# Attention scores by seven products, with their sums accumulated in two kept PSUM banks, a fused sum and maximum on VectorE, and one more pair of tiles

## The chip, the cores and the metric

The kernel runs on one core of one Trainium2 chip. The metric is the device time of one execution in microseconds (us). The engines are PE (TensorE, matrix products into PSUM), DVE (VectorE), ACT (ScalarE), POOL (GpSimd) and SP, whose queue issues most DMAs. Each engine works through its own instructions in order and waits at semaphores for the others. [...]

## The reference

The input x has 2 sequences of 2048 tokens with 512 features. With xn = layernorm(x), the output is

```
x + attention(xn) * silu(moe(xn))
```

`attention` normalises again, forms q, k, v with a 512x1536 matrix, takes causal softmax(q k^T / sqrt(512)) v with one head of width 512, multiplies by o_proj and adds its input. `moe` sends each token to the best 2 of 8 experts (512 to 352 to 512, with silu) and adds the two results with their softmax weights. All is fp32.

## The kernel before, in words

There are three stages: projections of all tokens with the expert routing, the experts, and the attention with the output. The change touches the third and the places where the second and third take PSUM banks.

The whole program is emitted under a manual schedule: every engine's instructions stand in the order in which the Python code emits them. So the order of the calls is the order of the queues, and it is by reading the calls that one sees what stands behind what.

**Attention.** A tile is 128 queries; there are 32, taken in the order `seq` (step number s = 0 to 31): the first sequence from its last tile to its first, then the second sequence in a mixed order. The keys of a sequence lie in 4 blocks of 512, and a tile needs the blocks up to its own, the last one masked. A chunk (s, j) is the scores of tile s against block j: `chunk_scores` (L1214) multiplies over the 512 features in 4 parts, masks the diagonal (L1224) and takes the row maximum (`maximum`, L1204). `end_scores` (L1305) makes nm, the negated maximum over a tile's chunks. `exponentials` (L1377) then runs exp on ACT for each piece, straight from the PSUM bank of a chunk or from the SBUF tile `turned[s]`, and sums the rows on the way. The exponentials are transposed by a split copy on POOL (L1394, `pu`), a DMA transpose (L1400, `puT`) and a join on DVE (`join_p`, L1414); the shortest tiles (`by_te`, at most 3x128 keys) are transposed on PE instead (`turn_p`, L1407), into a bank of kind "a".

**Seven products.** For pairs of tiles in `SCORED` (s//2 in 0, 1, 2, 3, 13, 14, 15), the scores of two tiles against blocks 0 and 1 are done by the Winograd form of Strassen's scheme: 2x2 parts, 7 products instead of 8, in `fast_scores` (L1254). It needs sums of the queries (`query_sums`, L1232, 4 sums in tile `sq`) and of the key blocks (`block_sums`, L1243, 4 sums in tile `tk`, once per sequence). Each product is two fp32 matmuls of 128x512 (the profile shows 4 PE instructions) into a bank of its own; the sums of products are made by DVE (L1277) in `turned[s]` and `turned[s+1]`, whose first 1024 columns are c11, c12 and c21, c22. The copy of product 1 is on ACT (L1290), at s=2 on DVE (L1288). `others` emits work that the caller hands in, such as `attended` and `join_p`.

**PSUM.** Two pools: `ps_b` with 3 banks, `ps_a` with 5, each used in turn. "a" holds the chunks (kept until their exponentials), PE's transposes and the experts' first products; "b" the values and the experts' second products. The products of `fast_scores` take from both.

**Around it.** In a step s the main loop emits, in this order where they apply: late work of earlier tiles (`attended`, ACT L1595 and DVE L1598), the sums of the next pair's queries, `fast_scores`, the chunks, joins, `values(s-2)` with `turn_p(s-1)`, `end_scores`, `combine_p`, `divisor` (L1556, waits for the exponentials of tile s-1), `exponentials`, the DMAs of `fetch_parts`, the work in `later` (`block_sums` and `combine_v` for the second sequence), the value products (`FAST` pairs use seven products here too), and, in odd steps from 3 on, `gate` (L1582: two ACT scalings L1587, two DVE sums L1588, a Silu L1590).

Of the kernel before, what the change touches and what calls it, by code (L numbers as in the profile page):

```python
# [20 lines left out]
P = 128  # L21
# [5 lines left out]
def gated_attention_moe(  # L27
# [962 lines left out]
    def up(i):  # L990
        ev = experts[i] = expert(places(i)[0][1], mybir.EngineType.PE)
        xT = xts.pop(i)
        ph = ps_a.tile([P, TB], F32, name=f"ph_{i}", tag="a")[:, :H]
# [40 lines left out]
    def up_pair(i, meanwhile):  # L1034
        ev = experts[i] = experts[i + 1] = expert(order[i], mybir.EngineType.PE)
        (a11, a12), (_, a22) = ([xts[i + k][:, 2 * j : 2 * j + 2] for j in range(2)] for k in range(2))
        s1, s2, s3, s4 = xsums.pop(i)
        hs = [hp.tile([P, H], F32, name=f"h_{i + k}", tag="h") for k in range(2)]
        (c11, c12), (c21, c22) = ([h[:, ts(j, H2)] for j in range(2)] for h in hs)

        def b(r, j):
            return lambda c: w1[0][:, bass.ds(ev, 1), 2 * r + c, ts(j, H2)]

        def t(k):
            return lambda c: w1s[0][:, bass.ds(ev, 1), k - 1, c, :]

        def made(x, y):
            ps = ps_a.tile([P, TB], F32, name="p7", tag="a")[:, :H2]
# [49 lines left out]
    def down(i):  # L1098
        ht = hts.pop(i)
        ev = experts.pop(i)  # L1100
        py = ps_b.tile([P, D], F32, name=f"py_{i}", tag="b")
# [78 lines left out]
    OUT = 4  # L1180


    SCORED = (0, 1, 2, 3, 13, 14, 15)
    FAST = SCORED + (4,)

    def place(s):
        b, t = divmod(seq[s], BT)
# [2 lines left out]
    def begin_scores(s):  # L1190
        b, t, first = place(s)
        widths[s] = [TB] * (b - first) + [(t + 1) * P]
        mx = sm.tile([P, NBB], F32, name=f"mx_{s}", tag="mx")
        nm = sm.tile([P, 1], F32, name=f"nm_{s}", tag="nm")
        scored[s] = mx, nm, []

    def room(s):

# [2 lines left out]
        )  # L1201
        turned[s] = tp.tile([P, longest], F32, name=f"pT_{s}", tag=f"pT{s % 4}", bufs=1)

    def maximum(s, src, at):  # L1204

        mx, _, pieces = scored[s]
        nc.vector.tensor_reduce(mx[:, len(pieces) : len(pieces) + 1], src, AX.X, ALU.max)
        pieces.append((src, at))

    def direct(s):  # L1210

        return range(2 if s // 2 in SCORED else 0, len(widths[s]))

    def chunk_scores(s, j):  # L1214
        b, t, first = place(s)
        w = widths[s][j]
        ps = ps_a.tile([P, TB], F32, name=f"ps_{s}_{j}", tag="a")
        for c in range(ND):
            nc.tensor.matmul(  # L1219
                ps[:, :w], lhsT=aqs[seq[s] // 2][:, c, ts(t % 2, P)], rhs=aks[first + j][:, c, :w],  # L1220
                start=(c == 0), stop=(c == ND - 1),
            )
        if first + j == b:
            nc.vector.tensor_tensor(ps[:, w - P : w], ps[:, w - P : w], keep, ALU.min)  # L1224
        maximum(s, ps[:, :w], j * TB)

# [24 lines left out]
                engine = nc.gpsimd if i == 3 and first == 0 else nc.vector  # L1251
                engine.tensor_tensor(k[:, i - 1], x1, x2, ALU.subtract)

    def fast_scores(s, pools, meanwhile=()):  # L1254

        first = place(s)[2]
        (a11, a12), (a21, a22) = (
# [3 lines left out]
        q, k = qsums.pop(s), bsums[first]  # L1261
        (c11, c12), (c21, c22) = ([turned[s + i][:, ts(j, TB)] for j in range(2)] for i in range(2))
        meanwhile = list(meanwhile)
        count = [0]

        def made(x, y):
            pool, tag = pools[count[0] % len(pools)]
            count[0] += 1
            ps = pool.tile([P, TB], F32, name=f"p7_{s}_{count[0]}", tag=tag)
            for c in range(ND // 2):  # L1270
                nc.tensor.matmul(  # L1271
                    ps, lhsT=x[:, c], rhs=y[:, c], start=(c == 0), stop=(c == ND // 2 - 1)
                )
            return ps

        def add(out, x, y):
            nc.vector.tensor_tensor(out, x, y, ALU.add)  # L1277

        def others(n):
            while meanwhile and n:  # L1280
# [1 line left out]
                f(*args)  # L1282
                n -= 1

        p1 = made(a11, b11)
        if s == 2:

            nc.vector.tensor_copy(c11, p1)  # L1288
        else:
            nc.scalar.copy(c11, p1)  # L1290
        p2 = made(a12, b21)
        add(c12, made(q[:, 1], k[:, 1]), c11)
        add(c11, p2, c11)
        add(c21, made(q[:, 2], k[:, 2]), c12)
        p5 = made(q[:, 0], k[:, 0])
        add(c22, p5, c21)
        add(c12, p5, c12)
        others(1)
        add(c12, made(q[:, 3], b22), c12)
        maximum(s, turned[s][:, : 2 * TB], 0)  # L1300
        others(1)
        add(c21, made(a22, k[:, 3]), c21)
        others(len(meanwhile))

    def end_scores(s):  # L1305
        mx, nm, pieces = scored[s]
        nc.vector.tensor_reduce(nm, mx[:, : len(pieces)], AX.X, ALU.max, negate=True)  # L1307

    for i in range(-5, 0):
        experts_step(i)  # L1310
# [8 lines left out]
    sm = right(att, name="sm2", bufs=4)  # L1319
    pairs_st = ExitStack()  # L1320
    wsp = right(pairs_st, name="wsp", bufs=1)
    ps_b = psum(att, name="ps_b", bufs=3, reuse_waits="tile")
    ps_a = psum(att, name="ps_a", bufs=5, reuse_waits="tile")

    keep = sm.tile([P, P], F32, name="keep", tag="keep", bufs=1)
    nc.gpsimd.memset(keep, HUGE)
# [32 lines left out]
    copy_w2(NS - DOWN)  # L1359
    for s in range(2):  # L1360
        begin_scores(s)
    for j in direct(0):
        chunk_scores(0, j)
    for i in range(NS, NS + DOWN + 2):
        experts_step(i)
    st.close()
    wp.close()

# [7 lines left out]

    def exponentials(s):  # L1377

        _, nm, pieces = scored.pop(s)
# [26 lines left out]

    def turn_p(s):  # L1407
        n = sum(widths[s])
        pt = ps_a.tile([P, TB], F32, name=f"pt_{s}", tag="a")
# [9 lines left out]
        )  # L1419

    def values(s):
        po = ps_b.tile([P, D], F32, name=f"po_{s}", tag="b")
        product(po, s, 0, place_keys(s), slice(0, D))
        outs[s] = po

# [64 lines left out]
        return lambda k: avs[place(s)[2] + k // 2][:, 2 * (k % 2) + half, cols]  # L1490

    def bank(s, name):
        return ps_b.tile([P, D], F32, name=f"{name}_{s}", tag="b")

    def half_d(s, name):
        return cp.tile([P, D // 2], F32, name=f"{name}_{s}", tag=name)
# [148 lines left out]
    later = {}  # L1645
    for steps, f, b in (
        ((10, 10, 11, 11), combine_v, K + 2), ((12, 12, 13, 13), combine_v, K + 1),
        ((20, 21, 22, 23), block_sums, K), ((24, 25, 26, 27), combine_v, K),
    ):
        for i, step in enumerate(steps):  # L1650
            later.setdefault(step, []).append((f, b, (i + 1,)))
# [7 lines left out]
    for s in range(NT + OUT + 2):  # L1659
# [41 lines left out]
        chunks = []  # L1701
        if s < NT and s != 1:
            chunks = [(k, j) for k in ((1,) if s == 0 else (s,)) for j in direct(k)]
        if s == 0:

            for k, j in chunks:
                chunk_scores(k, j)
            chunks = []
        if s < NT and s % 2 == 0 and len(pair) == 2:
            pools = [(ps_a, "a")] * 5 + [(ps_b, "b"), (ps_a, "a")]  # L1710
            if s < 3:
                pools = [(ps_b, "b")] * 3 + [(ps_a, "a")]
# [127 lines left out]
```

## Time and profile before

| what | before |
|---|---|
| median of 3 runs | 1022.91 us (1021.89 to 1023.93) |
| the profiled execution's own time | 1024.79 us |
| its span in the profile | 1023.1 us |
| PE busy | 1013.5 us (99%) |
| DVE busy | 712.2 us (70%) |
| ACT busy | 408.9 us (40%) |
| POOL busy | 482.1 us (47%) |
| PE clock granted | 0.999 of full |

The span runs from the first to the last instruction of the profiled execution; its own time also counts what lies around them. A row of a group gives line, engine, operation, tiles and shape, count, then busy time and mean ns of one, then the idle time of the engine before such instructions with what ended it. A row of waits gives who waited, for whom, us in total, times, and the longest. A row of the timeline gives start, duration, engine, line and operation, with consecutive like instructions merged ("x8"), and in brackets the idle time before with its releaser. Matmuls overlap, so the mean duration of one is longer than the distance from one start to the next. "PEld" is PE's loading of the stationary operand, which runs beside the products. Busy shares of engines other than the one that never rests say little by themselves.

### The profile page before, as it was taken

Reading aid. Unit: us, or ns where it says so; the run is one execution under the profiler, and the core shown is the slowest. Engines: PE = TensorE matmul, PEld = TensorE weight load, DVE = VectorE, ACT = ScalarE, POOL = GpSimd, SP = SyncE. Lnnn points to the kernel's source line nnn. Section 1 sums busy time; section 2 is a strip of 40 time slices with the busy share of each in tenths; the row PEclk is TensorE's granted clock in tenths of the full one; section 3 lists DMA queues with packets and bytes.
Section 4 is the critical chain, followed back from the end, with each engine's and each line's share of the span. In section 5 each row is a group of like instructions: output and inputs, shape, how many; then the busy total and the mean of one; then the engine's idle time right before and its main releaser. Section 6 shows DMA issues by size and latency. Waiting matters only on the chain.

```text
span 1023.1 us, 13492 instructions
## 1 busy us (share of the span) xinstructions
PE 1013.5 (99%) x3956; PEld 666.2 (65%) x3956; DVE 712.2 (70%) x1395; ACT 408.9 (40%) x817; POOL 482.1 (47%) x479
## 2 busy tenths in 40 slices
PE   9999999999999999999999999999999999999998
PEld 4688888864666766676654447677675544447577
DVE  5777746896777777767734659778576556888667
ACT  3344445322454445444445222132345454542341
POOL 3364564003644444444431247164556776754272
PEclk9999999999999999999999999999999999999999
DMA  8799986989999999999999567454768769653371
GB/s 300 203 252 296 303 264 248 341 283 198 206 220 221 213 212 211 219 216 212 209 201 246 155 205 157 105 143 144 192 181 235 215 196 254 184 135 111 98 162 42
DMA packets 299367, 209.42 MB, mean 205 GB/s; under 512 B 234392, under 2 KB 247448, under 8 KB 298272
## 3 DMA queue, kind: packets, MB, share of 16 engines
q1 hardware_dynamic: 283840, 156.09, 61.7%
q0 software_dynamic: 10560, 35.17, 12.8%
q10 hardware_dynamic: 4896, 17.30, 4.6%
q8 instruction: 34, 0.56, 0.2%
q14 instruction: 37, 0.30, 0.1%
HBM read 92.89 MB, written 60.03 MB: 149 GB/s over the span
## 4 chain that ended last, share of the span: by engine, by line
PE 89%; DMA 4%; issue 3%; DVE 2%; POOL 1%; ACT 1%; SPq 1%; POOLq 0%; DVEq 0%; ACTq 0%
PE py L1107 15%; PE ps L1219 12%; PE p L1482 12%; PE p L1050 10%; PE p L1271 8%; PE po L1434 6%; PE bank_a L465 5%; PE bank_b L465 5%; PE bank_c L465 5%; PE p L1434 3%; PE bank_d L465 2%; PE ph L998 2%; DMA y_d<-y 1%; DMA raw<-in_qkv_t_dram 1%; PE pg L347 1%
## 5 line engine op out<-in xcount | busy, mean ns | idle before, releaser
L1107 PE MATMUL py<-arena,ht 128*128 (+3 forms) x408 | 182.3, 593 | 0.0
L1219 PE MATMUL ps<-k,q 128*128 128x512 f32 (+3 forms) x416 | 143.0, 495 | 0.0
L1394 POOL COPY pu<-pT 128x1024 uint16<-128x1024 uint16 (+2 forms) x74 | 82.5, 1147 | 119.4 <-ACT pT L1384 59.5
L1078 POOL COPY hu<-h 128x704 uint16<-128x704 uint16 x68 | 63.5, 953 | 154.6 <-issue 119.9
L1107 PEld LDWEIGHTS py<-arena,ht 128*128 128x128 f32 (+3 forms) x408 | 73.2, 183 | 82.1 <-issue 77.0
L1219 PEld LDWEIGHTS ps<-k,q 128*128 128x128 f32 x416 | 74.6, 190 | 66.8 <-issue 57.4
L883 POOL DMA_INDIRECT xs<-zu_d,toki x68 | 81.0, 1191 | 70.8 <-DVE toki L731 55.9
L1093 ACT ACTIVATE ht<-ht,b1sel 128x128 f32<-128x128 f32 (+3 forms) x228 | 71.1, 378 | 97.1 <-DVE ht L1087 97.1
L1057 DVE TENSOR_TENSOR h<-p,h 128x176 f32<-128x176 f32 x182 | 55.5, 337 | 60.8 <-PE p L1050 57.2
L1577 POOL DMA_INDIRECT yg<-y_d,posi x64 | 67.7, 1058 | 36.0 <-DVE yg L1588 20.5
L1434 PE MATMUL po<-v,pT 128*128 128x512 f32 x152 | 67.9, 593 | 0.4 <-DVE pT L1416 0.4
L280 POOL COPY zu<-z 128x1024 uint16<-128x1024 uint16 x32 | 37.5, 1173 | 61.3 <-DVE z L265 61.3
L1416 DVE COPY pT<-puT 128x1024 uint16<-128x1024 uint16 (+2 forms) x74 | 54.0, 757 | 10.3 <-DMA puT<-pu 10.2
L1384 ACT ACTIVATE pT<-pT,nm 128x1024 f32<-128x1024 f32 x14 | 16.1, 1148 | 110.2 <-DVE nm L1307 71.2
L1115 ACT COPY y<-py 128x512 f32<-128x512 f32 x55 | 32.2, 585 | 62.7 <-PE py L1107 48.1
L1384 ACT ACTIVATE pT<-ps,nm 128x512 f32<-128x512 f32 (+3 forms) x52 | 30.0, 581 | 64.5 <-DVE nm L1307 40.8
L1277 DVE TENSOR_TENSOR pT<-p,pT 128x512 f32<-128x512 f32 x49 | 32.9, 686 | 25.9 <-PE p L1271 22.2
L1434 PEld LDWEIGHTS po<-v,pT 128*128 128x128 f32 x152 | 28.5, 190 | 32.6 <-issue 30.9
L958 DVE COPY xT<-xhT 128x1024 uint16<-128x1024 uint16 x68 | 46.6, 709 | 4.3 <-DMA xhT<-xs 4.1
L1606 POOL TENSOR_TENSOR o<-o,yg 128x512 f32<-128x512 f32 x30 | 42.0, 1399 | 14.3 <-DVE o L1598 14.2
L1598 DVE SCALAR_TENSOR_TENSOR o<-xo,xscale,o 128x512 f32<-128x512 f32 x30 | 27.3, 918 | 28.7 <-ACT o L1595 28.7
L1087 DVE COPY ht<-huT 128x768 uint16<-128x768 uint16 x68 | 38.7, 569 | 10.3 <-DMA huT<-hu 10.2
(323 smaller groups left out, 2155.4 us busy)
## 6 DMA issues: line engine op xcount, KB each, us to landing
y_d<-y SPq DMA_DIRECT2D x68, 256.0 KB, 4.6
zu_d<-zu SPq DMA_DIRECT2D x32, 264.0 KB, 3.2
kt_d<-kT ACTq DMA_DIRECT2D x8, 1024.0 KB
k<-kt_d SPq DMA_DIRECT2D x32, 256.0 KB, 4.9
q<-qt_d SPq DMA_DIRECT2D x32, 256.0 KB, 5.3
v<-v_d SPq DMA_DIRECT2D x32, 256.0 KB, 4.7
xo<-in_x_dram SPq DMA_DIRECT2D x32, 256.0 KB, 4.0
x<-in_x_dram SPq DMA_DIRECT2D x30, 256.0 KB, 5.3
```

The source lines that it names most:

```text
L465: nc.tensor.matmul(ps[:, r, :], lhsT=lhs[:, c, ts(r, P)], rhs=rhs[:, c, :], start=(start and r + c == 0), stop=(c == 1), skip_group_check= ...
L883: nc.gpsimd.indirect_dma_start(out=xs, out_offset=None, in_=zu_d, in_offset=bass.IndirectOffsetOnAxis(ap=toki[:, order[i] : order[i] + 1], ...
L1050: nc.tensor.matmul(ps, lhsT=x[:, c], rhs=y(c).rearrange("p o h -> p (o h)"), start=(c == 0), stop=(c == ND // 2 - 1),)
L1078: nc.gpsimd.tensor_copy(hu[:, :, :H], h.bitcast(U16).rearrange("p (d h) -> p h d", h=2))
L1093: nc.scalar.activation(ht[:hn, c, at], ht[:hn, c, at], AF.Silu, bias=b1sel[:hn, c, j : j + 1])
L1107: nc.tensor.matmul(py[at, :], lhsT=ht[:k, c, at], rhs=rhs[n], start=(c == 0), stop=(c == NH - 1),)
L1219: nc.tensor.matmul(ps[:, :w], lhsT=aqs[seq[s] // 2][:, c, ts(t % 2, P)], rhs=aks[first + j][:, c, :w], start=(c == 0), stop=(c == ND - 1),)
L1271: nc.tensor.matmul(ps, lhsT=x[:, c], rhs=y[:, c], start=(c == 0), stop=(c == ND // 2 - 1))
L1394: nc.gpsimd.tensor_copy(pu[:, : 2 * w].rearrange("p (h d) -> p h d", h=2), turned[s][:, k : k + w].bitcast(U16).rearrange("p (d h) -> p h ...
L1434: nc.tensor.matmul(dst, lhsT=turned[s][:, ts(k, P)], rhs=avs[first + k // BT][:, k % BT, cols], start=(start and k == k0), stop=(k == k1 - 1),
L1482: nc.tensor.matmul(dst, lhsT=a[:, k], rhs=v(k), start=(k == 0), stop=(stop and k == n - 1))
L1577: nc.gpsimd.indirect_dma_start(out=y, out_offset=None, in_=y_d, in_offset=bass.IndirectOffsetOnAxis(ap=posi[k][:, n : n + 1], axis=0),)
```

## The change

- In `fast_scores` the sums move to PE. Two banks (0 and 1, `seeds`) are kept for the whole attention stage and never allotted again. Product 1 goes to bank_a and is copied to bank_b; product 2 is accumulated onto bank_a, which then is c11; product 6 onto bank_b, which is copied to bank_c; product 7 onto bank_c, product 3 onto bank_b, and, when bank_c has been read, product 4 onto bank_c, which then is c21. Product 5 goes to bank_d and is copied to c22. Copies are on ACT, three of them on DVE at s=2.
- Two sums are left for DVE, c12 = bank_b + product 5 and c22 = bank_c + product 5, and they are done by `tensor_tensor_reduce`, which also gives the row maximum. c11 and c21 get a maximum of 512 columns each.
- The order of the products becomes 1, 5, 2, 6, a chunk of the tile (`filling`), 7, 3, 4.
- One more pair, 8 (s = 16 and 17), is scored by seven products; its values are not (`FAST` is now written out). The sums of the second sequence's key blocks move from steps 20 to 23 to steps 14 and 15.
- The banks are handed out one by one by `bank_of`, in turn within a kind: 3 for "b" and 5 for "a" as before during the experts; from the attention on, 3 for "b" (2, 3, 4) and 3 for "a" (5, 6, 7).
- At s=0 the two chunks of tile 1 no longer stand ahead of `fast_scores`: one is its filling, the other follows it.

The diff, without the lines that only replace `ps_a.tile` or `ps_b.tile` by `bank_of` (in `up`, `up_pair`, `down`, `turn_p`, `values`, `bank`) and without those that unpack the longer list in `scored`:

```diff
-    SCORED = (0, 1, 2, 3, 13, 14, 15)
-    FAST = SCORED + (4,)
+    SCORED = (0, 1, 2, 3, 8, 13, 14, 15)
+    FAST = (0, 1, 2, 3, 4, 13, 14, 15)
...
-        scored[s] = mx, nm, []
+        scored[s] = [mx, nm, [], 0]
...
-    def maximum(s, src, at):
-
-        mx, _, pieces = scored[s]
-        nc.vector.tensor_reduce(mx[:, len(pieces) : len(pieces) + 1], src, AX.X, ALU.max)
-        pieces.append((src, at))
+    def next_max(s):
+        scored[s][3] += 1
+        return scored[s][0][:, scored[s][3] - 1 : scored[s][3]]
+
+    def maximum(s, src):
+
+        nc.vector.tensor_reduce(next_max(s), src, AX.X, ALU.max)
...
-    def chunk_scores(s, j):
+    def chunk_scores(s, j, kind="a"):
...
-        ps = ps_a.tile([P, TB], F32, name=f"ps_{s}_{j}", tag="a")
+        ps = bank_of(kind, f"ps_{s}_{j}")
...
-        maximum(s, ps[:, :w], j * TB)
+        maximum(s, ps[:, :w])
+        scored[s][2].append((ps[:, :w], j * TB))
...
-    def fast_scores(s, pools, meanwhile=()):
+    def fast_scores(s, kind, between, meanwhile=()):
...
-        count = [0]
-
-        def made(x, y):
-            pool, tag = pools[count[0] % len(pools)]
-            count[0] += 1
-            ps = pool.tile([P, TB], F32, name=f"p7_{s}_{count[0]}", tag=tag)
+        bank_a, bank_d = bank_of(kind, f"sa_{s}"), bank_of(kind, f"sd_{s}")
+        bank_b, bank_c = seeds
+        copy = nc.vector.tensor_copy if s == 2 else nc.scalar.copy
+
+        def made(ps, x, y, start=False):
             for c in range(ND // 2):
                 nc.tensor.matmul(
-                    ps, lhsT=x[:, c], rhs=y[:, c], start=(c == 0), stop=(c == ND // 2 - 1)
+                    ps, lhsT=x[:, c], rhs=y[:, c], start=(start and c == 0),
+                    stop=(c == ND // 2 - 1), skip_group_check=True,
                 )
-            return ps
-
-        def add(out, x, y):
-            nc.vector.tensor_tensor(out, x, y, ALU.add)
+
+        def add(i, out, x):
+            nc.vector.tensor_tensor_reduce(
+                out=out, in0=x, in1=c22, scale=1.0, scalar=-HUGE, op0=ALU.add, op1=ALU.max,
+                accum_out=next_max(s + i),
+            )
...
-        p1 = made(a11, b11)
-        if s == 2:
-
-            nc.vector.tensor_copy(c11, p1)
-        else:
-            nc.scalar.copy(c11, p1)
-        p2 = made(a12, b21)
-        add(c12, made(q[:, 1], k[:, 1]), c11)
-        add(c11, p2, c11)
-        add(c21, made(q[:, 2], k[:, 2]), c12)
-        p5 = made(q[:, 0], k[:, 0])
-        add(c22, p5, c21)
-        add(c12, p5, c12)
+        made(bank_a, a11, b11, start=True)
+        copy(bank_b, bank_a)
+        made(bank_d, q[:, 0], k[:, 0], start=True)
+        copy(c22, bank_d)
+        made(bank_a, a12, b21)
+        nc.scalar.copy(c11, bank_a)
+        made(bank_b, q[:, 1], k[:, 1])
+        copy(bank_c, bank_b)
+        maximum(s, c11)
         others(1)
-        add(c12, made(q[:, 3], b22), c12)
-        maximum(s, turned[s][:, : 2 * TB], 0)
+        for f, *args in between:
+            f(*args)
+        made(bank_c, q[:, 2], k[:, 2])
+        made(bank_b, q[:, 3], b22)
+        add(0, c12, bank_b)
+        scored[s][2].insert(0, (turned[s][:, : 2 * TB], 0))
+        add(1, c22, bank_c)
         others(1)
-        add(c21, made(a22, k[:, 3]), c21)
+        made(bank_c, a22, k[:, 3])
+        nc.scalar.copy(c21, bank_c)
+        scored[s + 1][2].insert(0, (turned[s + 1][:, : 2 * TB], 0))
         others(len(meanwhile))
...
-    ps_b = psum(att, name="ps_b", bufs=3, reuse_waits="tile")
-    ps_a = psum(att, name="ps_a", bufs=5, reuse_waits="tile")
+    ps = psum(att, name="ps", bufs=1, reuse_waits="tile")
+    turns = {"b": [0, 1, 2], "a": [3, 4, 5, 6, 7]}
+
+    def bank_of(kind, name):
+        n = turns[kind].pop(0)
+        turns[kind].append(n)
+        return ps.tile([P, TB], F32, name=name, tag=f"bank{n}")
...
+    turns["a"] = [5, 6, 7]
     for j in direct(0):
         chunk_scores(0, j)
     for i in range(NS, NS + DOWN + 2):
         experts_step(i)
+    turns["b"] = [2, 3, 4]
+    seeds = [ps.tile([P, TB], F32, name=f"seed{n}", tag=f"bank{n}") for n in range(2)]
...
-        ((20, 21, 22, 23), block_sums, K), ((24, 25, 26, 27), combine_v, K),
+        ((14, 14, 15, 15), block_sums, K), ((24, 25, 26, 27), combine_v, K),
...
-        if s == 0:
-
-            for k, j in chunks:
-                chunk_scores(k, j)
-            chunks = []
         if s < NT and s % 2 == 0 and len(pair) == 2:
-            pools = [(ps_a, "a")] * 5 + [(ps_b, "b"), (ps_a, "a")]
-            if s < 3:
-                pools = [(ps_b, "b")] * 3 + [(ps_a, "a")]
+            filling = [(chunk_scores, *chunks.pop(0))]
...
-            fast_scores(s, pools, late + joins[:now])
+            fast_scores(s, "b" if s < 3 else "a", filling, late + joins[:now])
...
-            chunk_scores(k, j)
+            chunk_scores(k, j, "b" if s == 0 else "a")
...
-                maximum(s + 1, turned[s + 1][:, : 2 * TB], 0)
+                maximum(s + 1, turned[s + 1][:, :TB])
```

More of the change, by code (lines that the diff above doesn't have):

```diff
@@ L992, in up @@
         xT = xts.pop(i)
-        ph = ps_a.tile([P, TB], F32, name=f"ph_{i}", tag="a")[:, :H]
+        ph = bank_of("a", f"ph_{i}")[:, :H]
         for c in range(ND):
@@ L1047, in made @@
         def made(x, y):
-            ps = ps_a.tile([P, TB], F32, name="p7", tag="a")[:, :H2]
+            ps = bank_of("a", "p7")[:, :H2]
             for c in range(ND // 2):
@@ L1100, in down @@
         ev = experts.pop(i)
-        py = ps_b.tile([P, D], F32, name=f"py_{i}", tag="b")
+        py = bank_of("b", f"py_{i}")
         for c, (_, hn) in enumerate(HCH):
@@ L1283, in others @@
                 n -= 1
-        p1 = made(a11, b11)
-        if s == 2:
-            nc.vector.tensor_copy(c11, p1)
-        else:
-            nc.scalar.copy(c11, p1)
-        p2 = made(a12, b21)
-        add(c12, made(q[:, 1], k[:, 1]), c11)
-        add(c11, p2, c11)
-        add(c21, made(q[:, 2], k[:, 2]), c12)
-        p5 = made(q[:, 0], k[:, 0])
-        add(c22, p5, c21)
-        add(c12, p5, c12)
-        others(1)
-        add(c12, made(q[:, 3], b22), c12)
-        maximum(s, turned[s][:, : 2 * TB], 0)
+        made(bank_a, a11, b11, start=True)
[7 more added lines that the diff above has]
+        maximum(s, c11)
+        others(1)
+        for f, *args in between:
[5 more added lines that the diff above has]
+        add(1, c22, bank_c)
         others(1)
-        add(c21, made(a22, k[:, 3]), c21)
+        made(bank_c, a22, k[:, 3])
+        nc.scalar.copy(c21, bank_c)
+        scored[s + 1][2].insert(0, (turned[s + 1][:, : 2 * TB], 0))
         others(len(meanwhile))
     def end_scores(s):
-        mx, nm, pieces = scored[s]
-        nc.vector.tensor_reduce(nm, mx[:, : len(pieces)], AX.X, ALU.max, negate=True)
+        mx, nm, _, n = scored[s]
+        nc.vector.tensor_reduce(nm, mx[:, :n], AX.X, ALU.max, negate=True)
     for i in range(-5, 0):
@@ L1377, in exponentials @@
     def exponentials(s):
-        _, nm, pieces = scored.pop(s)
+        _, nm, pieces, _ = scored.pop(s)
         rs = sm.tile([P, NBB], F32, name=f"rs_{s}", tag="rs")
@@ L1408, in turn_p @@
         n = sum(widths[s])
-        pt = ps_a.tile([P, TB], F32, name=f"pt_{s}", tag="a")
+        pt = bank_of("a", f"pt_{s}")
         for k in range(n // P):
@@ L1421, in values @@
     def values(s):
-        po = ps_b.tile([P, D], F32, name=f"po_{s}", tag="b")
+        po = bank_of("b", f"po_{s}")
         product(po, s, 0, place_keys(s), slice(0, D))
@@ L1492, in bank @@
     def bank(s, name):
-        return ps_b.tile([P, D], F32, name=f"{name}_{s}", tag="b")
+        return bank_of("b", f"{name}_{s}")
     def half_d(s, name):
```

## The prediction

> **What bounds the kernel now.** I read the page first (engine shares, then the chain), then the groups by shape, then PE's waits, then the timeline around each place that the change touches.
>
> The page, part 1; PE's share of the span is the thing to see:
> ```profile
> PE 1013.5 (99%) x3956; PEld 666.2 (65%) x3956; DVE 712.2 (70%) x1395; ACT 408.9 (40%) x817; POOL 482.1 (47%) x479
> ```
> All of PE's waits come to under 6 us; two of the nine lines:
> ```profile
> PE bank_b L465 <- ACT bank_c L494: 0.7, 1, 0.7
> PE po L1434 <- DVE pT L1416: 0.4, 1, 0.4
> ```
> So PE runs back to back and is the bound: an idle microsecond put into its queue is a microsecond of span. Groups by shape (busy, mean ns, then idle before):
> ```profile
> L1271 PE MATMUL p<-tk,sq 128*128 128x512 f32 x84 | 37.2, 592 | 0.0
> L1277 DVE TENSOR_TENSOR pT<-p,pT 128x512 f32<-128x512 f32 x49 | 32.9, 686 | 25.9 <-PE p L1271 22.2 <-ACT pT L1290 3.3
> ```
> The second line is the slack that is at stake: DVE and ACT reach the products late or early as they like, because each product has a bank of its own. The timeline of step s=26 and the start of s=2 (start, duration) shows how late:
> ```profile
> 882.37 3.60 PE L1271 MATMUL p<-k,q 128*128 128x512 f32 x8
> 885.81 5.31 PE L1271 MATMUL p<-tk,sq 128*128 128x512 f32 x12
> 889.45 1.06 ACT L1590 ACTIVATE yg<-yg 128x1024 f32<-128x1024 f32 x1
> 890.41 0.57 ACT L1290 COPY pT<-p 128x512 f32<-128x512 f32 x1
> 891.01 3.40 DVE L1277 TENSOR_TENSOR pT<-p,pT 128x512 f32<-128x512 f32 x5 [1.69 <-ACT pT L1290]
> ...
> 602.47 3.60 PE L1271 MATMUL p<-k,q 128*128 128x512 f32 x8
> 606.20 0.16 DVE L1558 TENSOR_REDUCE ri<-rs 128x1 f32<-128x3 f32 x1 [1.26 <-ACT pT L1384]
> 606.47 0.67 DVE L1288 COPY pT<-p 128x512 f32<-128x512 f32 x1
> ```
> Product 1 of s=26 is issued by 884.1, yet its copy runs at 890.4, behind the gate's Silu in ACT's queue; PE never notices. Four instructions make a product; eight start from 882.37 to 885.81, so a product is 1.72 us.
>
> [...]
>
> **The change, part by part.**
>
> *Saved on PE.* Pair 8 (s=16, 17) takes 7 products for 8: −1.72 us. The other seven pairs keep theirs.
>
> *Order on PE.* Before: products 1, 2, 6, 7, 5, 3, 4, each with a fresh bank. After: 1 (bank_a), 5 (bank_d), 2 (bank_a), 6 (bank_b), one chunk, 7 (bank_c), 3 (bank_b), 4 (bank_c). Four of them add onto what a copy or an earlier product left, so four points of PE's queue now depend on ACT or DVE. Two are covered: product 6 stands behind product 2, which has waited for the same copy; product 7 needs bank_b→bank_c, some 0.16+0.57+0.1=0.83 us after product 6, under the chunk of 3.44 us (8 instructions of 0.43; at s=16 it is 128 wide, 8×0.13=1.05, still enough; without it each pair would wait 0.83). The other two, products 2 and 4, are waits 2 and 1 below.
>
> *Lighter queues.* Per pair DVE loses seven adds (0.69) and two maxima of 1024 (1.21), gains two sums with maximum and two maxima of 512 (0.68, half of 1024's stream): 4.5 us less, worth nothing by itself, since PE hides it all. ACT gains four copies of 0.57 a pair, nothing by themselves either; uncovered they are the waits below.
>
> *New wait 1, product 4.* It adds into bank_c, which add(1) must have read; add(1) is behind add(0), as add(1) overwrites c22; add(0) needs product 3, the product just ahead of product 4. No PE work is between. Wait: 0.16 (last end against next issue slot: 0.59 less 0.43) + 2×0.69 + some 0.1 of hops = 1.65 us; ×8 = 13.2. The fused instruction is not in the trace: at least 0.69 (same stream; shorter is excluded, since it reads as much), at most two passes, 1.21 as the 1024 maximum[...] I take 0.69. Chunk, values and everything later on PE queue behind.
>
> *New wait 2, product 2.* It adds into bank_a, so the copy bank_a→bank_b must be done; only product 5 (1.72) covers it. The copy is due 3.43 after product 1 starts (602.47→605.91). From ACT's L1290 and DVE's L1288 in before: at s=4 and 6 done 0.2 late; s=26: 890.98 against 885.81, 5.2; s=28: 917.55 against 913.28, 4.3, of which some 0.3 is made good by the waits before, 4.0; s=30: 0.2. The lateness at s=26 and 28 is no accident of one run's order: the Silu of the gate waits for two sums on DVE (L1588), DVE is behind query_sums and joins that POOL slows (the four sums at s=25 took 1.25, 0.50, 1.48 and 1.48), and none of that is changed. At s=0 product 5 now comes second and wants k[:,0], ready at 586.26: 0.3. At s=2 DVE copies, behind divisor(0), which needs exponentials(0); nm(0) now needs chunk (1,3), the last PE work of step 0: 1.2 + 2.5 (three exponentials) + 0.35 + 0.67 = 4.9, so 1.5. At s=16 the gate of step 15 is ahead in ACT, and DVE ahead of it gets block_sums (4×1.22, moved from steps 20 to 23, where they were hidden) and query_sums(16) (4×0.42, up to 4×1.04 beside POOL): 6.6 to 9.1, less 2.8 of idle time there. These lines set the place:
> ```profile
> 793.25 7.92 PE L1219 MATMUL ps<-k,q 128*128 128x512 f32 x24
> 795.70 1.83 DVE L1588 SCALAR_TENSOR_TENSOR yg<-yg,share,yg 128x512 f32<-128x512 f32 x2 [0.88 <-ACT yg L1587]
> 797.59 1.06 ACT L1590 ACTIVATE yg<-yg 128x1024 f32<-128x1024 f32 x1
> ```
> Silu ends at 798.65+5.0=803.6, the copy at 804.2, due 796.7: 7.5. Sum 0.3+1.5+0.2+0.2+7.5+5.2+4.0+0.2 = 19.1. SP sees only earlier reads: the keys of block K land by 788, before step 14's sums; the queries of s=16 are fetched at 785.75.
>
> *New wait 3, three "a" banks for five.* Counting the turns, two chunks meet a bank still unread. (3,3) gets the bank of (2,2), whose exponential follows nm(2), and nm(2) stands on DVE behind a mask, a maximum and six joins: 0.7 + 6×0.9 (L1416's mean is 0.83, more beside POOL) + 0.2 = 6.3 after chunk (2,3), while PE has only chunk (3,2), 3.4, to do: 2.9 late, and 1.13 + 0.68 of exponentials: 4.7. In before the same order stands there and nm(2) came 2 us after PE had finished (3,3); with five banks that was free. (21,0) gets that of (20,0): 841.70 against 839.07, 2.7.
> ```profile
> 626.02 0.14 DVE L1307 TENSOR_REDUCE nm<-mx 128x1 f32<-128x3 f32 x1
> 839.07 4.46 PE L1219 MATMUL ps<-k,q 128*128 128x512 f32 x10
> 841.01 0.69 ACT L1384 ACTIVATE pT<-ps,nm 128x512 f32<-128x512 f32 x1
> ```
> All other turns have over 1 us in hand.
>
> *New wait 4, values(16).* exp(16) was in pieces of 512 while chunk (17,·) ran 8.6 us; now it is one piece after product 4: copy and transpose copy 2.1, table load 1.28, exponential 1.15, POOL copy 1.24, transpose 3.3, join 0.83 = 9.9; PE has 5.3 (values(14), values(15), two chunks): 4.6.
>
> Sum: 13.2 + 19.1 + 7.4 + 4.6 − 1.7 = +42.6 us. On the profiled execution, 1024.79 with a span of 1023.1, that is 1067.4; on the median, 1022.91, it is 1065.5. I say 1065. A measurement here tells 0.2%, 2 us, from no change.
>
> **Rivals.**
>
> *Product 4's wait alone (0.22):* DVE and ACT, lighter and given time by each stall, catch up, and waits 2 to 4 shrink to a tenth: 13.2−1.7+3.1: 1037.5. For: the 4.5 us less DVE work a pair. Against: the late copies hang on Silu, nm and exponentials, whose queues hold no fast_scores work.
>
> *Dearer (0.13):* the fused instruction makes two passes, 16×0.52=8.3[...] 1065+15: 1080.[...]
>
> *Not slower, the other side (0.04):* add(1) ends before product 4 is due, at one place, product 4, since a pair without waits gains 1.72 once: 1021.2. It decides where the waits of all pairs together are under 1.7, 0.2 a pair. Two adds of 0.69 behind product 3 speak against it.
>
> *The likeliest (0.61):* all four waits as worked out, 1065, own range 1050 to 1078.
>
> **How the numbers follow.** The range 1036 to 1083 takes in the likeliest with the bounds of its sizes (fused instruction to 1.21, s=16 from 4 to 10), nearly all of the dear case's and the upper half of product 4 alone. Faster 0.03, within 0.2% 0.01, slower 0.96.
>
> **What would show it.** PE's waits: product 4 on DVE's fused instruction, eight times, near 1.65; product 2 on the copies, longest at s=16, 26, 28; chunks on exponentials at s=3 and 21; values on the join at s=18. PE's busy share falls from 99% to about 95. I am wrong if the fused row is far from 0.69, if PE's idle time lies elsewhere, or if the copies move ahead of Silu.

## The result and the profile after

| what | before | after |
|---|---|---|
| median | 1022.9 us | 1086.1 us (1082.9 to 1087.9, 4 runs) |
| ratio to before | | 1.0614, 95% interval 1.0584 to 1.0645 |
| the profiled execution's own time / its span | 1024.79 / 1023.1 us | 1084.66 / 1083.0 us |
| PE busy / idle in the span | 1013.5 / 9.6 us | 1029.4 / 53.6 us |
| PE clock granted | 0.999 | 0.986 |

The change makes the kernel 6.1% slower, 21 us more than the 1065 predicted and just above the range (1036 to 1083). First the page of the changed kernel, part 1:

```profile
PE 1029.4 (95%) x3952; PEld 667.1 (62%) x3952; DVE 680.9 (63%) x1382; ACT 425.2 (39%) x844; POOL 472.2 (44%) x479
```

PE runs four instructions fewer than before and is busy 15.9 us longer, and it idles 44.0 us more. The span grew by the two together, 59.9 us. PE's waits in the changed kernel (who waited, for whom, us in total, times, longest):

```profile
PE seed L1273 <- DVE mx L1279: 12.2, 8, 1.5
PE sd L1273 <- ACT pT L1400: 7.9, 2, 5.6
PE ps L1221 <- ACT pT L1400: 6.9, 3, 3.6
PE sa L1273 <- ACT seed L1291: 5.5, 3, 3.4
PE po L1450 <- DVE pT L1432: 4.5, 1, 4.5
PE p L1498 <- DVE o L1515: 3.8, 1, 3.8
PE sa L1273 <- DVE seed L1291: 2.8, 1, 2.8
```

Every line is new, and they sum to 43.6 us: product 4 behind the fused instruction (first line), product 5 on a bank whose exponential is late (second), chunks on exponentials, product 2 on the copy of product 1 (fourth and last), values(16), and the end of the kernel. The fused instruction's row among the groups by shape (busy, mean ns of one, idle before):

```profile
L1279 DVE CUSTOM_DVE_ANT_0 pT<-seed,pT 128x512 f32<-128x512 f32 x16 | 11.1, 691 | 20.4 <-PE seed L1273 20.1
```

The timeline of s=16 on PE (start, duration, then the wait in brackets):

```profile
811.80 1.88 PE L1273 MATMUL sa<-k,q 128*128 128x512 f32 x4
819.26 3.78 PE L1273 MATMUL sd<-tk,sq 128*128 128x512 f32 x4 [5.58 <-ACT pT L1400]
824.18 1.98 PE L1273 MATMUL sa<-k,q 128*128 128x512 f32 x4 [1.14 <-ACT seed L1291]
826.00 1.88 PE L1273 MATMUL seed<-tk,sq 128*128 128x512 f32 x4
...
833.77 1.98 PE L1273 MATMUL seed<-tk,q 128*128 128x512 f32 x4 [1.53 <-DVE mx L1279]
```

The first is one pass, 0.69 us. In the second two things are to be seen. A product's four instructions take 1.88 us, but 3.78 after the wait of 5.58: half the rate; the granted clock is 0.50 of full from 816.72 to 823.55 us. And after the waits of 1.14 and 1.53 they take 1.98, only 0.10 more. Measured against 0.43 us for each instruction of 512 columns (and in proportion for fewer), seven waits of the changed kernel are followed by a stretch at half rate, and the time lost there is 1.80 at s=2, 1.76 at chunk (3,3), 1.90 at s=16, 2.23 at values(16), 1.80 at chunk (21,0), 1.74 at s=26 and 1.77 at s=28. That is 13.0 us. Two smaller things come with each wait. After the other twelve of the 19 new waits the first instruction takes 0.10 longer: 1.2. And ahead of each of the 19 the last instruction counts 0.16 more: an instruction of 512 columns lasts 0.59 and the next starts 0.43 after it, so 0.16 lie under the next one, unless that one has to wait: 3.0. Together this is 17.2 of the 17.6 us by which PE's busy time exceeds what the saved product leaves (15.9+1.7). So a wait of this kernel cost some 0.26 more than the idle time that the list gives for it, before any loss of rate.

### The profile page after: what moved, and what is told of

Same layout as the page of the kernel before. It is cut to its first block, busy times and chain, and to the rows that moved or that the text cites. A ratio compares the mean times of both kernels' runs of the same rounds, so it can differ in the third digit from the quotient of the medians.

```text
span 1083.0 us, 13483 instructions
## 1 busy us (share of the span) xinstructions
PE 1029.4 (95%) x3952; PEld 667.1 (62%) x3952; DVE 680.9 (63%) x1382; ACT 425.2 (39%) x844; POOL 472.2 (44%) x479
## 5 line engine op out<-in xcount | busy, mean ns | idle before, releaser
L1410 POOL COPY pu<-pT 128x1024 uint16<-128x1024 uint16 (+2 forms) x74 | 75.0, 1044 | 172.5 <-ACT pT L1400 100.4
L1221 PE MATMUL ps<-k,q 128*128 128x512 f32 (+3 forms) x384 | 132.9, 495 | 6.9 <-ACT pT L1400 6.9
L1221 PEld LDWEIGHTS ps<-k,q 128*128 128x128 f32 x384 | 70.0, 195 | 68.2 <-issue 50.2
L1450 PE MATMUL po<-v,pT 128*128 128x512 f32 x152 | 70.1, 608 | 4.5 <-DVE pT L1432 4.5
L1432 DVE COPY pT<-puT 128x1024 uint16<-128x1024 uint16 (+2 forms) x74 | 51.0, 725 | 8.5 <-DMA puT<-pu 8.5
L1400 ACT ACTIVATE pT<-ps,nm 128x512 f32<-128x512 f32 (+3 forms) x48 | 27.2, 570 | 55.6 <-DVE nm L1315 32.0
L1210 DVE TENSOR_REDUCE mx<-ps 128x1 f32<-128x512 f32 (+3 forms) x48 | 26.7, 557 | 26.1 <-PE ps L1221 25.0
L1623 POOL TENSOR_TENSOR o<-o,xo 128x512 f32<-128x512 f32 x30 | 41.9, 1395 | 2.4
```

The costliest lines, as they stand in the source:

```text
L1221: nc.tensor.matmul(ps[:, :w], lhsT=aqs[seq[s] // 2][:, c, ts(t % 2, P)], rhs=aks[first + j][:, c, :w], start=(c == 0), stop=(c == ND - 1),)
L1410: nc.gpsimd.tensor_copy(pu[:, : 2 * w].rearrange("p (h d) -> p h d", h=2), turned[s][:, k : k + w].bitcast(U16).rearrange("p (d h) -> p h ...
L1432: nc.vector.tensor_copy(turned[s][:, k : k + w].bitcast(U16).rearrange("p (i t h) -> p i t h", t=P, h=2), puT[:, : 2 * w // P, :].rearrang ...
L1450: nc.tensor.matmul(dst, lhsT=turned[s][:, ts(k, P)], rhs=avs[first + k // BT][:, k % BT, cols], start=(start and k == k0), stop=(k == k1 - 1),
```

## The experiments

Theory P is the prediction's account. T, N and C are what the trace of the changed kernel adds to it: what steps 16 to 19 lost in it (T), a late row maximum rather than the gate at s=16 and 26 (N), half rate of PE after long waits (C). Times are medians; ratios are to the kernel before, run beside them.

**Each new wait by itself: product 4.** A second copy of product 5 lets the sum on bank_c run beside product 3.

```diff
+        nc.scalar.copy(c12, bank_d)
...
         made(bank_c, q[:, 2], k[:, 2])
+        add(1, c22, bank_c)
         made(bank_b, q[:, 3], b22)
         add(0, c12, bank_b)
-        add(1, c22, bank_c)
```

> Product 5 is copied a second time, to c12 (one more ACT copy of 0.57 us per pair), so that the sum on bank_c needs nothing of product 3 and runs while product 3 runs. Theory P: product 4's wait of 1.5 to 1.65 goes at eight places, and the 0.1 that PE loses after each: 1086.1 less 13.0 = 1073. Rival A (DVE is late for other reasons, so the wait stays in part): half of it, 1080. Rival B (these waits also cost PE's rate afterwards, 1.7 each): 1086.1 less 26 = 1060.

Measured 1076.7, ratio 1.0519 (1.0502 to 1.0537): 9.4 less than the changed kernel, between theory P and rival A. All eight waits are gone from the list. What was lost again stands in the timeline of s=3:

```profile
620.95 5.32 PE L1221 MATMUL ps<-k,q 128*128 128x256 f32 x16
632.81 2.08 PE L1221 MATMUL ps<-k,q 128*128 128x128 f32 x8 [6.54 <-ACT pT L1401]
```

Chunk (3,3) waited 3.62 in the changed kernel and waits 6.54 now. Its bank is freed by an exponential that hangs on DVE's joins, so PE arriving earlier only waits longer: the gain of the two product-4 waits ahead of it (3.3 us) is swallowed in the main. And product 2 at s=26 waits 2.54 for 0.91, as product 5 ahead of it ran at full rate here and the copy came no earlier.

**Other banks.** Only the allotment of three banks changes.

```diff
-            chunk_scores(k, j, "b" if s == 0 else "a")
+            chunk_scores(k, j, "b" if s == 0 or (k, j) in ((3, 3), (21, 0)) else "a")
...
+        if s == NT - 2:
+            turns["b"][:2] = turns["b"][1::-1]
         p57 = bank(s, "p57")
```

> Three allotments change and nothing else: chunks (3,3) and (21,0) take the next bank of kind b, and at the end the product p57(30) takes the bank of p03(28) instead of that of p64(28). Theory C (each wait of over 2 us is followed by a stretch at half PE rate): 3.6+1.8 at s=3, 2.6+1.8 at s=21, 3.8 at the end: 13.6 less than 1086.1, 1072.5. Theory W (the waits alone): 3.6+2.6+3.8 = 10.0 less, 1076. Rival: other work meets the same banks and waits instead: 1080 or more.

Measured 1071.5, ratio 1.0457 (1.0419 to 1.0495), 14.6 less; the three waits are gone and nothing else waits instead. The median lies nearer to C (13.6) than to W (10.0), but it does not decide: the interval is some 4 us to either side, the profiled spans differ by 10.9 only, and PE's busy time is the same in both (1029.6 and 1029.4), so in that execution half rate turned up at other waits. The granted clock differs between the four executions, too: 0.994 and 0.992 in those of 1067.3 and 1069.2 us, 0.983 in those of 1073.8 and 1076.3. The third edit settles the end of the kernel: `bank_of` gives p57(30) a bank by turn whose last reader, an add, stands behind four joins, `combine_p` and the gate's sums in DVE's queue.

**Both together**, to see whether the swallowed part comes back.

> The edits of other_banks and p4_free together. Additive reading: 14.6 and 9.4 less than 1086.1, 1062. Elastic reading (in p4_free the wait of chunk (3,3) grew from 3.6 to 6.5 and swallowed what the two product-4 waits of s=0 and s=2 had given; with another bank that wait is gone, so they count too): 14.6 and 13.0 less, 1058.5, and step 4 starts some 8 us earlier than in the changed kernel.

Measured 1058.4, ratio 1.0340 (1.0304 to 1.0376): the elastic reading. From the start of s=0 to that of s=4 the changed kernel takes 78.05 us, with product 4 freed 76.40, with other banks 72.52, with both 68.74: freeing product 4 gives 1.65 alone and 3.78 once the wait behind it is gone.

**The gate.** Is the copy of product 1 late because of the gate's Silu? The first try moved the whole gate, and with it the tile's output and the next gathers.

```diff
+            if s in (16, 26, 28):
+                gate(s - 4)
+                emit(s - 4)
+                gather_y(s - 2)
```

(after `fast_scores`; taken out at their old places)

> The gate of the tiles (scalings, sums, Silu), their output and the next gather are emitted after the seven products at s=16, 26 and 28 instead of ahead of them. Theory P (the copy of product 1 is late because it stands behind the gate's Silu, 7.5+5.2+4.0): 16.7 less, 1069.4. Theory N (at s=16 and 26 the row maximum is late behind sums on VectorE, and with three a banks product 5 waits for the exponential that needs it; the gate adds only 1.1 and 0.9 there; at s=28 it is the cause, 3.4 and 1.7 of half rate after it): 7.1 less, 1079.

Measured 1097.1, ratio 1.0732 (1.0692 to 1.0771): slower by 11, which neither theory said. At s=28 product 2 now waits 5.91 instead of 3.43. POOL's and then DVE's timeline there:

```profile
950.48 1.36 POOL L1622 TENSOR_TENSOR o<-o,yg 128x512 f32<-128x512 f32 x1 [17.64 <-ACT yg L1606]
951.91 1.27 POOL L1623 TENSOR_TENSOR o<-o,xo 128x512 f32<-128x512 f32 x1
953.34 1.01 POOL L1593 DMA_INDIRECT yg<-y_d,posi  x1 [0.15 <-issue]
954.65 1.13 POOL L1593 DMA_INDIRECT yg<-y_d,posi  x1 [0.30 <-issue]
956.09 1.16 POOL L1593 DMA_INDIRECT yg<-y_d,posi  x1 [0.30 <-issue]
957.55 0.95 POOL L1593 DMA_INDIRECT yg<-y_d,posi  x1 [0.30 <-DVE mx L1210]
958.50 2.78 POOL L1410 COPY pu<-pT 128x1024 uint16<-128x1024 uint16 x3
```
```profile
963.05 1.98 DVE L1432 COPY pT<-puT 128x1024 uint16<-128x1024 uint16 x2 [5.69 <-DMA puT<-pu]
965.23 0.56 DVE L1432 COPY pT<-puT 128x768 uint16<-128x768 uint16 x1 [0.20 <-DMA puT<-pu]
965.71 0.15 DVE L1315 TENSOR_REDUCE nm<-mx 128x1 f32<-128x3 f32 x1
```

POOL waits for the later Silu, issues the output and four gathers, and only then splits the exponentials; their joins on DVE come later, the row maximum behind the joins too, and the exponential and the copy after it. At s=18 values(16) waits 8.2 for its join instead of 4.5. My edit moved three queues while it meant to move one, so its time says nothing on the question. One thing in its trace does: with the gate out of the way product 5 still waits 5.58 at s=16 and 2.26 at s=26, as N has it.

**The copy alone past the gate.** Product 1 and its copy are emitted at the end of the step before; PE's order is the same and POOL's untouched.

```diff
+        if s + 1 in (16, 26, 28):
+            start_scores(s + 1, "a")    # product 1 and copy(bank_b, bank_a)
         for k in range(0, NT - 2, 2):
             ...
                 gate(k)
```

> At s=16, 26 and 28 product 1 and its copy to bank_b are emitted at the end of the step before, ahead of the gate; PE's order stays as it was, on ACT only this one copy passes the gate, and POOL's queue is untouched (in gate_later the output and four gathers were moved with the gate). Theory P (the copy stands behind Silu, 7.5+5.2+4.0): 16.7 less than the changed kernel's 1086.1, 1069.4. Theory N (at s=16 and 26 the row maximum on VectorE is late and bank_d is still unread; Silu costs only 1.3 and 1.0 there, at s=28 3.4 and the 2.2 of half rate after it): 7.9 less, 1078.

Measured 1078.7, ratio 1.0534 (1.0494 to 1.0574): N, 7.4 less. At s=28 no wait is left; at s=16 product 5 waits 5.58 and at s=26 2.27, exactly as before the edit. There the gate was second in line. DVE and ACT of the changed kernel at the end of step 15:

```profile
809.41 2.17 DVE L1255 TENSOR_TENSOR tk<-k,k 128x1024 f32<-128x1024 f32 x1
811.62 2.17 DVE L1255 TENSOR_TENSOR tk<-k,tk 128x1024 f32<-128x1024 f32 x1
813.72 1.75 DVE L1614 SCALAR_TENSOR_TENSOR o<-xo,xscale,o 128x512 f32<-128x512 f32 x1
815.38 1.48 DVE L1241 TENSOR_TENSOR sq<-q 128x256 f32<-128x256 f32 x1
...
818.56 0.15 DVE L1315 TENSOR_REDUCE nm<-mx 128x1 f32<-128x1 f32 x1
```
```profile
818.75 0.37 ACT L1400 ACTIVATE pT<-ps,nm 128x128 f32<-128x128 f32 x1 [6.33 <-DVE nm L1315]
```

The sums of keys and queries stand ahead of the row maximum (818.56), the exponential waits for that, and bank_d, one of three, is the bank it reads.

**The sums behind the maximum**, added to the first, flawed edit of the gate: at s=15 and 25 `query_sums`, at s=15 also the second key sum, come after `end_scores`.

> As gate_later, and at s=15 and 25 the next pair's query sums, at s=15 also the second key sum, stand behind the row maximum on VectorE instead of ahead of it. Theory N: the exponentials and with them bank_d come 4.4 us earlier at s=16 and 4.9 at s=26 with the half rate after it: 1086.1 less 17.4 = 1069 (1066 to 1074), 10 below gate_later. Theory P: the gate was the cause, so within 2 us of gate_later.

Measured 1091.5, ratio 1.0661 (1.0634 to 1.0688), 5.6 below gate_later where N expected 10 and P at most 2. Product 5's wait fell from 5.58 to 1.1 at s=16, where it now is for its own query sum, and from 2.3 to 1.7 at s=26; values(16) still waits 8.2. The direction is N's, the size about half of it.

**Pair 8 taken out.**

```diff
-    SCORED = (0, 1, 2, 3, 8, 13, 14, 15)
+    SCORED = (0, 1, 2, 3, 13, 14, 15)
...
-        pt = bank_of("a", f"pt_{s}")
+        pt = bank_of("b" if s == 15 else "a", f"pt_{s}")
...
-        ((14, 14, 15, 15), block_sums, K), ((24, 25, 26, 27), combine_v, K),
+        ((20, 21, 22, 23), block_sums, K), ((24, 25, 26, 27), combine_v, K),
```

> Pair 8 is scored by chunks again and the key sums go back to steps 20 to 23; the transposes of step 15 take a bank of kind b, as three a banks would otherwise wait in a circle. Theory P (the prediction's steps): the waits at s=16 (7.5), of product 4 (1.65) and of values(16) (4.6) go, 1.7 of PE work returns: 12.0 less than the changed kernel's 1086.1, 1074. Theory T (what the trace of the changed kernel shows for steps 16 to 19): these steps lost 16.4 us over before, so 1070 to 1071. Rival: with three a banks the chunks of tile 17 each wait for an exponential of tile 16, which gives most of it back: 1080 or more.

Measured 1076.2, ratio 1.0524 (1.0498 to 1.0550), 9.9 less: three fifths of what the steps 16 to 19 had lost. The chunks of tile 17 now wait 2.5 for an exponential of tile 16, with half rate after it, and chunk (18,0) 1.1, so the rival is partly right.

**Pair 8 alone in the kernel before**, in its old scheme with a bank for each product. The edit is the list `SCORED` (and `FAST` written out) and the steps of `block_sums`.

> The kernel before with pair 8 added to the pairs that are scored by seven products, in the scheme of before (a bank for each product, the sums on VectorE), and the key sums in steps 14 and 15. Theory P: PE saves one product of 1.72 us and no wait is exposed: 1022.9 less 1.7 = 1021.2, ratio 0.9983. Rival: the sums of keys and queries that delay VectorE at s=16 hold up a bank there: 1023 to 1027.

Measured 1033.5, ratio 1.0093 (1.0075 to 1.0110): slower, against theory P and worse than the rival. PE around s=16 to 18:

```profile
790.81 3.60 PE L1271 MATMUL p<-k,q 128*128 128x512 f32 x8
796.39 1.98 PE L1271 MATMUL p<-tk,sq 128*128 128x512 f32 x4 [1.98 <-DVE sq L1239]
799.25 3.67 PE L1271 MATMUL p<-tk,sq 128*128 128x512 f32 x8 [0.88 <-DVE tk L1252]
...
818.65 5.71 PE L1434 MATMUL po<-v,pT 128*128 128x512 f32 x9 [6.09 <-issue]
```

2.0 for a query sum, 0.9 for a key sum, 6.1 at values(16), whose joins on DVE begin at 817.0, and 1.7 of half rate after it, less 1.7: 9.0 of the measured 9.5 (0.93% of 1022.9). So most of the loss around s=16 belongs to the extra pair, not to the banks: the sums have no time there, and tile 16's exponentials start only when the sums of the products are made, with too little PE work behind them. One saved product does not pay for that in either scheme.

**The fused instruction alone in the kernel before.**

```diff
-        add(c12, made(q[:, 3], b22), c12)
-        maximum(s, turned[s][:, : 2 * TB], 0)
+        nc.vector.tensor_tensor_reduce(
+            out=c12, in0=made(q[:, 3], b22), in1=c12, scale=1.0, scalar=-HUGE,
+            op0=ALU.add, op1=ALU.max, accum_out=mx[:, 3:4],
+        )
+        # maximum of c11, and a 128x1 maximum of the two
```

> The kernel before with one part of the change alone: the last sum of c12 and its row maximum in one VectorE instruction, the maximum of c11 apart, and a 128x1 maximum to join the two; some 0.4 us less VectorE time per pair. Theory P: nothing, 1022.9 within 0.2%, as PE hides all of it. Rival: VectorE's queue is what bounds some step around the products, so up to 7 x 0.4 = 2.8 less, 1020.

Measured 1022.9, ratio 1.0000 (0.9983 to 1.0017): nothing, as P says.

**Idle time and PE's rate.** The kernel before, with PE held up between two chunks.

```diff
             chunk_scores(k, j)
             ...
+            if j == 0 and k == s:
+                aq = aqs[seq[s] // 2][:, :, ts(seq[s] % 2, P)]
+                for _ in range(HOLD.get(s, 0)):
+                    nc.vector.tensor_copy(aq, aq)
```

> The kernel before, with PE held up at nine places: between the first and second chunk of steps 9, 10, 11, 12, 20, 22, 23, 24 and 25 VectorE copies the queries onto themselves 1, 2, 3, 4, 2, 5, 1, 7 and 3 times. Theory C: places that idle under about 2 us lose just the idle time, longer ones some 1.7 more whatever their length; with an estimated 0.6 per copy and 0.8 around them 24+8.5 above 1023, 1055. Rival: only the idle time is lost, 1047; or the loss grows with the idle time.

One run, 1062.6, where C had 1055 and the rival 1047. Six places waited, 27.7 us in all instead of 24; PE's busy time grew by 9.8, and 27.7+9.8 is all of the span's growth (37.8) but 0.3. The shortest wait and the two longest, each with the chunk behind it (384, 384 and 128 wide, at full rate 2.74, 2.74 and 1.05):

```profile
738.88 2.85 PE L1219 MATMUL ps<-k,q 128*128 128x384 f32 x8 [1.72 <-DVE q L1729]
...
853.18 4.50 PE L1219 MATMUL ps<-k,q 128*128 128x384 f32 x8 [6.23 <-DVE q L1729]
...
901.16 2.08 PE L1219 MATMUL ps<-k,q 128*128 128x128 f32 x8 [9.89 <-DVE q L1729]
903.04 3.39 PE L1434 MATMUL po<-v,pT 128*128 128x512 f32 x6
```

After 1.72 and 2.78 us of idle time nothing is lost, after 3.41, 3.69, 6.23 and 9.89 some 1.8, 2.7, 1.8 and 1.7: a price that did not grow with the length here. This is theory C, but a wait of over 2 us is not enough for it: the one of 2.78 cost nothing. The last section has what decides.

**PE kept busy in the waits.** Products that nobody reads, into bank_c, ahead of the instructions that wait.

```diff
+        warm(s, {16: 3, 26: 1}.get(s, 0))    # n products into bank_c
         made(bank_d, q[:, 0], k[:, 0], start=True)
```

(and likewise at s=2 and 28, ahead of (3,3), (21,0) and values(16))

> Eleven more products (44 PE instructions, 1.72 us each product, 18.9 us of PE work) whose results nobody reads are put into bank_c just ahead of the instructions that wait: one at s=2, two ahead of chunk (3,3), three at s=16, two ahead of values(16), one at s=21, 26 and 28. Each fits into its wait. Theory C (PE drops to half rate after an idle time of over 2 us, about 1.7 to 2.2 lost at each of seven places): 1.85+1.8+1.9+2.2+1.8+1.74+1.67 = 13.0 less, 1073, and a granted clock near full. Rival (the rate afterwards has nothing to do with PE being idle): 1086, or longer by what does not fit.

Measured 1083.8, ratio 1.0584 (1.0556 to 1.0612). Only 2.3 less: the miss teaches most. The granted clock did rise, to 0.993, and 44 more instructions (18.9 us) raised PE's busy time by 13.8 only. But at s=16:

```profile
813.62 5.31 PE L1318 MATMUL seed<-k,q 128*128 128x512 f32 x12
819.38 1.98 PE L1273 MATMUL sd<-tk,sq 128*128 128x512 f32 x4 [0.44 <-ACT pT L1411]
824.31 3.40 PE L1273 MATMUL sa<-k,q 128*128 128x512 f32 x4 [2.94 <-ACT seed L1291]
```

Product 5 runs at full rate, and product 2 still cannot start before 824.3, since the copy it waits for hangs on the row maximum; the time that product 5 lost at half rate had been covered by that second wait. Now PE idles 2.94 there and runs slowly afterwards. The same holds at s=2: from its first product to chunk (3,3) PE takes 31.0 us in the changed kernel and 31.2 here. In no_pair8, too, PE kept its rate after the 2.83 at s=2, and chunk (3,3) started 31.2 after that first product all the same, having waited 5.49. So at these two places the slow stretch ahead of a second late wait cost nothing, and the 13.0 us are not all to be had. Besides, the wait of p57(30) at the end, 3.69, was followed by half rate here and lost 3.1; in the changed kernel 3.75 at this place had lost nothing more.

**All of it together**: other banks, product 4, the copy past the gate, the sums behind the maximum.

> The edits of banks_p4 and copy_first, and at s=15 and 25 the query sums (at s=15 also the second key sum) behind the row maximum. If the waits named are all there is, what is left over the kernel before is values(16) (4.5 and 2.2 of half rate), the copy at s=2 (2.8 and up to 1.9) and small ones, less 1.7: 1034; with waits that move to the next late engine, as in gate_later: 1043. Slower than before in both cases (1022.9).

Measured 1045.6, ratio 1.0222 (1.0176 to 1.0269), the second forecast. What is left: values(16) 4.5, a new wait of 3.2 of product 7 for its copy at s=16 (now behind the Silu), the copy at s=2 2.5, product 5 1.6 and 1.1, and half rate after the longer ones. No version ran faster than the kernel before, and none could by much: PE is busy for 99% of that kernel's span.

## Why the prediction was wrong

By its own steps:

- *What bounds the kernel* and the direction were right. PE's new idle time is 44.0 us where the waits of the sum made 44.3 (42.6+1.7), but that they meet so closely is in part luck: a wait of 3.8 at the end that nobody had foreseen makes up for waits that were put too high.
- *Wait 1*: right. 12.2 of idle time for 13.2, in which the working counted eight times the 0.16 that the profile books as busy. The fused instruction takes 0.69, with a readout of 0.08 behind it, not two passes.
- *Wait 2*: places right, 16.2 for 19.1 (8.3 of it waits of product 2, 7.9 waits of product 5 just ahead): 2.8 for 1.5 at s=2, 6.7 for 7.5 at s=16, 3.2 for 5.2 at s=26, 3.4 for 4.0 at s=28. At s=2 the terms add up to 4.7, not to the 4.9 given, which makes the size there worse. The cause was right at s=2 and 28. At s=16 and 26 it was incomplete: the lateness came through DVE's sums, nm and the exponential to bank_d first, the gate adding 1 us behind that (copy_first). The small ones at s=0, 4, 6 and 30 did not show.
- *Wait 3*: 3.62 for 4.7, 2.61 for 2.7. "All other turns have over 1 us in hand" was wrong: chunk (18,0) waits 0.7, and the turn of kind "b" at the end gives p57(30) an unread bank, 3.75.
- *Wait 4*: 4.50 for 4.6.
- *Saved on PE*: 1.72 of work, but this was not set against what pair 8 itself costs, which stood spread over waits 1, 2 and 4. Alone, in the old scheme, it costs 9.5 (before_pair8).
- *Lighter queues*: worth nothing, as said (before_fused).

The step that failed is the choice of the likeliest case: it priced an idle microsecond of PE at one microsecond and left dearer long stalls to the rival "dearer", with a chance of 0.13. What that rival's 15 us hold for stalls, beyond the 8.3 for two passes, was the author's estimate, which the trace of the kernel before did not show. Measured, half rate followed seven waits of the changed kernel and cost 1.74 to 2.23 at each, 13.0 in all. The length of a wait alone did not tell which: waits of 2.27, 2.61 and 2.83 are among the seven, and the one of 3.75 is not (last section). 1065+13.0+3.8 would have been 1082. The rival that DVE and ACT, being lighter, catch up fell: they wait on each other's results, not for time.

Open: how much of the 13.0 could be had back without moving the waits.

## What to carry to other kernels

Accumulating in PSUM turns sums that could come late into copies and reads that must come in time: list, for each accumulating product, the reader or writer of its bank, and what stands ahead of that on its queue. Where PE is the bound, price each uncovered stall by what the traces of the kernel show: here its length plus 0.26 us, and 1.74 to 2.23 more where half rate followed (after every wait of over 4 us in these traces, after some between 2 and 4, as the next section shows), except where another late wait came at once. Before an edit is tested, list each queue that it moves (here POOL's); and a saved stall shows only once the next wait behind it, on something that does not depend on PE, is gone.

## What had not been expected of the hardware

Over the traces of the changed kernel and the runs above, of 39 waits of PE of 3.4 us and more 37 were followed by a stretch at half rate (the 3.75 at the end of the changed kernel and 3.62 at the end of no_pair8 were not); of 24 waits between 2.5 and 3.0 us 17 were; of 9 between 2.1 and 2.3 us 4; after the single waits of 1.5 us none. The same wait went either way: chunk (21,0), 2.61 us, lost 1.80 in the changed kernel and nothing in copy_first. So in these traces length alone did not decide.

What went with the loss stands in their granted clock. In the changed kernel this is 0.50 in seven stretches before the end of the span, which start at 611.92, 635.82, 816.72, 844.03, 878.16, 925.95 and 963.50 us: 7, 60, 68, 78, 92 and 103 times 3.413 us after the first. Two of them last 6.83 us, the others 3.41. In the traces of the other runs, too, such stretches start a whole number of times 3.413 us apart and, but for the last one of the span, last one to five times that. So each trace can be laid out in windows of 3.413 us, at whose borders alone the granted clock was seen to change. Laid over chunk (21,0), in the changed kernel and then in copy_first (window, its length, PE's busy time and instructions, granted clock, DMA share and GB/s):

```profile
874.75:878.16 3.41, 1.38 (x3) 1.00 0.40 142
878.16:881.58 3.42, 3.42 (x5) 0.50 0.92 205
```
```profile
874.45:877.86 3.41, 2.34 (x8) 1.00 0.65 186
877.86:881.27 3.41, 1.88 (x5) 1.00 0.40 121
881.27:884.69 3.42, 3.42 (x10) 1.00 0.88 198
```

In the first PE idles 2.03 us of one window, and the next is at half rate. In the second the same wait falls on two windows, 1.07 and 1.53 of idle time, and nothing follows. The other windows agree. In the changed kernel, after the first 5 us, eight windows at full rate have 2.03 to 3.41 us of idle time, and half rate followed each; after the eight with 1.51 to 1.92 it never did. In the traces of all runs 65 such windows have 2.0 us of idle time or more, and half rate followed each; of 52 with 1.5 to 2.0 it followed one (1.90, in gate_later). PE came back to full rate after a window with at most 0.56 us of idle time (0.51 at 820.14 in the changed kernel) and stayed at half after each with 0.70 or more (2.54 at 816.72). The wait of 3.75 at the end of the changed kernel fell on two windows as 1.92 and 1.83, and nothing more was lost. An estimate from these windows: a wait of 4 us or more puts 2 us or more into one of them wherever it starts; with a shorter one it depends on how it falls, and so on everything ahead of it. This was read from the traces afterwards; no run placed a wait on purpose to test it.
